# First attention of a vision tower: relu(q-k) by one add-and-clamp per four images, and matmuls in 32-column strips

## The chip, the cores and the metric

The kernel runs on one core of one Trainium2 chip. The core has five engines with a queue each: PE (TensorE, matrix products into PSUM), DVE (VectorE), ACT (ScalarE), POOL (GpSimd) and SP, which here only issues transfers. An engine takes its instructions strictly in the order in which the program gives them, and waits on semaphores for the other engines. The metric is the time of the whole program on the device in microseconds (us); the median of three runs counts.

## What is computed

The program is a small vision transformer: a tokenizer of two convolutions, a first layer (an attention and a feed-forward part that is itself an attention of experts), and a second layer (a linear attention and a mixture of experts). The change touches the first attention alone. For each of 128 images with 64 tokens of 256 features:

```python
Q = x @ Wq.T; K = x @ Wk.T; V = x @ Wv.T          # x: the layer norm of h
Qg = Q.reshape(B, L, 1, 8, 32)
Kg = K.reshape(B, 1, L, 8, 32)
diff = Qg - Kg                                     # every query against every key
attn = einsum('bqkgd,d->bqkg', relu(diff), w_mlp) + b_mlp[0]
attn = softmax(relu(attn), axis=2)                 # over the keys
out = einsum('bqkg,bkdg->bqdg', attn, Vg)
h = h + out
```

So for each image, query, key and group, 32 values relu(q - k) are weighted by `w_mlp` and summed. All is float32.

## The kernel before

`relu_attention` (L309) works on eight blocks of 16 images. In a block the features lie on the 128 partitions, in two halves (`hf`), and each image has its 64 tokens in the free dimension. A block is worked off in eight chunks of eight queries, which makes 64 chunks. For each chunk, half and image there is one part of 8 queries x 64 keys, 32 parts in all, and each must become relu(q - k) before PE sums it over features with the weights `wide` into the scores `sc` (`summed`, L340: a matmul of 32 columns, so that four images fill the four 32-row strips of `sc`).

The 32 parts are shared out by hand:

- VectorE makes 18 by `larger` (L529, the instruction is L532): max(q, k), for four images at once (2048 elements a partition, four times a chunk; the tile comes from the pool `amv` with three buffers) and once for two images (12 and 13 of half 1, 1024 elements, from `amg` with five buffers). q is read from PSUM (`pc`), broadcast over the keys; k from SBUF, broadcast over the queries.
- POOL and ACT make 12 by `difference` (L536): POOL subtracts (L540, 1024 elements, six times a chunk, `m` from `amg`), ACT clamps (L541). POOL reads a copy of q in SBUF (`queried`, L469).
- ACT makes two alone by `by_query` (L545, L550), relu(q - k) with q as the bias of one query at a time.

Since relu(q - k) = max(q, k) - k, the parts of VectorE lack a term in k. `key_sums` (L439) sums w times k over these parts once a block into `pkb`, `correction` (L449, L452) makes `kb` = b_mlp minus that sum, and `begin` (L521, L525) starts each chunk's `sc` with `kb`, by four matmuls of 32 columns with the identity as the stationary operand.

`less_max` (L562: a reduction at L566 and two more instructions, L567 and L568), `exponents`, `sums`, `weights` and `transpose` (L582, L589: 16 matmuls that turn `e` round, 64 columns each) finish the softmax of the chunk before, and lie among the steps of the present chunk. Keys (`keys`, L407), values (`values`, L426), queries (`queries`, L461) of a block are full 128-column matmuls; keys and values of the next block are made beside the chunks of the present one, each in four of eight chunks; queries are made for each next chunk.

The order of all of it is written out by hand at L696 to L757 under `manual_schedule`; `at(n, place, ...)` puts the side work (statistics and layer norm of the next block, its keys and values, the outcome of the last block with `outcome`, `back`, `added`, and in the last chunks the start of the next stage) into named places of chunk n. In one chunk VectorE has, in this order: max of images 0-3 and 4-7 of half 0, `less_max` of the chunk before, max of 0-3 of half 1, `sums`, max of 4-7 of half 1, max of 12 and 13 of half 1, and statistics. PE's sums stand behind the maxima and differences that feed them. `added` (L510) puts the result back into `h`.

Of the kernel before, what the change touches and what calls it, by code (L numbers as in the profile page):

```python
# [20 lines left out]
P = 128  # L21
B = 128
T = 64
D = 256
LN_EPS = 1e-5
BN_EPS = 1e-3
# [282 lines left out]
def relu_attention(c, sh, wqkv, wmlp, bmlp, beside):  # L309
# [10 lines left out]
    with (  # L320
# [24 lines left out]

        def direct(i, hf):

            return i // 4 == 2 or (i // 4 == 3 and (hf == 0 or i % 4 == 2))

        class Block:  # L350
# [52 lines left out]
            def keys(self, s, fo):  # L403

                self.ps["k", s, fo] = pk = sh.ps([P, 8, T], "pk")
                for fi in range(2):
                    nc.tensor.matmul(  # L407
                        pk.rearrange("p i t -> p (i t)"),
                        w[:, fi, D + fo * P : D + (fo + 1) * P],
                        self.xT[:, fi, 4 * s : 4 * s + 4, :].rearrange("p n t -> p (n t)"),  # L410
                        start=(fi == 0),
                        stop=(fi == 1),
                    )

            def keyed(self, s, fo, vector=False):
                if s == 0 and fo == 0:
                    self.k = bp.tile([P, 2, NB, T], F32, tag="k", name="k")
                copy = nc.vector.tensor_copy if vector else nc.scalar.copy
                copy(self.k[:, fo, 8 * s : 8 * s + 8], self.ps.pop(("k", s, fo)))  # L419

            def values(self, i):

                self.ps["v", i] = pv = sh.ps([P, 2, D], "pv")
                for j in range(2):
                    for fi in range(2):
                        nc.tensor.matmul(  # L426
                            pv[:, j],
                            self.xT[:, fi, 2 * i + j],
                            w[:, fi, 2 * D : 3 * D],
                            start=(fi == 0),  # L430
                            stop=(fi == 1),
                        )
# [5 lines left out]

            def key_sums(self):  # L439
                self.ps["b"] = pk = sh.ps([P, T], "pkb")  # L440
                for i0 in range(0, NB, 4):
                    for hf in range(2):
                        for i in range(i0, i0 + 4):
                            js = [(n, f) for n in range(i % 4, NB, 4) for f in range(2)]
                            js = [(n, f) for n, f in js if not direct(n // 2 * 2, f)]
                            if (i, hf) in js:
                                summed(pk, i, hf, self.k[:, hf, i], (i, hf) == js[0], (i, hf) == js[-1])

            def correction(self):  # L449

                self.kb = bp.tile([P, T], F32, tag="kb", name="kb")
                nc.vector.tensor_scalar(self.kb, self.ps.pop("b"), -1.0, bm, ALU.mult, ALU.add)  # L452

            def queries(self, q0):

                self.pc[q0] = pc = psc.tile([P, 2 * NB * 8 + 8], F32, tag="pc", name="pc")
                pq = pc[:, : 2 * NB * 8].rearrange("p (c i t) -> p c i t", c=2, i=NB)
                xi = self.xT.rearrange("p c n (b t) -> p c (n b) t", b=2)
                for fo in range(2):
                    for fi in range(2):  # L460
                        nc.tensor.matmul(  # L461
                            pq[:, fo],
                            w[:, fi, fo * P : (fo + 1) * P],
                            xi[:, fi, :, q0 : q0 + 8],
                            start=(fi == 0),
                            stop=(fi == 1),
                        )

            def queried(self, q0):  # L469
                self.q[q0] = q = ep.tile([P, 2, NB // 2, 8], F32, tag="q", name="q")  # L470
                pq = self.pc[q0][:, : 2 * NB * 8].rearrange("p (c i t) -> p c i t", c=2, i=NB)
                nc.scalar.copy(q, pq[:, :, NB // 2 :])  # L472

# [38 lines left out]
        class Chunk:  # L512


            def __init__(self, blk, q0):
                self.blk, self.q0, self.parts, self.m = blk, q0, {}, {}
                self.pc = blk.pc.pop(q0)
                self.pq = self.pc[:, : 2 * NB * 8].rearrange("p (c i t) -> p c i t", c=2, i=NB)
                self.q = blk.q.pop(q0)

            def begin(self):  # L521
                self.sc = pss.tile([P, 8, T], F32, tag="sc", name="sc")
                for j in range(0, P, 32):
                    j = slice(j, j + 32)
                    nc.tensor.matmul(  # L525
                        self.sc[j], c.ident[:, j], bcast(self.blk.kb, 1, 8), start=True, stop=False
                    )

            def larger(self, pool, i, n, hf):  # L529
                m = pool.tile([P, n, 8, T], F32, tag="m", name="m")  # L530
                k = bcast(self.blk.k[:, hf, i : i + n], 2, 8)
                nc.vector.tensor_tensor(m, bcast(self.pq[:, hf, i : i + n], 3, T), k, ALU.max)  # L532
                for j in range(n):
                    self.parts[i + j, hf] = m[:, j]

            def difference(self, i, hf):  # L536
                m = mgp.tile([P, 2, 8, T], F32, tag="m", name="m")
                s = i - NB // 2
# [22 lines left out]

            def less_max(self):  # L562
# [3 lines left out]
                nc.vector.tensor_reduce(pm, self.sc, AX.X, ALU.max)  # L566
                nc.vector.tensor_scalar_max(mx, pm, 0.0)  # L567
                nc.vector.scalar_tensor_tensor(  # L568
                    e, self.sc, 0.0, bcast(mx, 2, T), ALU.max, ALU.subtract
                )  # L570
# [11 lines left out]
            def transpose(self):  # L582
# [4 lines left out]
                for j in range(8):  # L587
                    for par in range(2):
                        nc.tensor.matmul(  # L589
                            pt[par * 64 : par * 64 + 64, j], self.e[:, j], rows[:, par], start=True, stop=True  # L590
                        )

# [34 lines left out]
        def first_rest(x):  # L627
            for s in range(2):
                x.keys(s, 1)
                x.keyed(s, 1, True)  # L630
            x.key_sums()
            x.correction()

        for b, x in enumerate(blocks):
# [43 lines left out]
            for fo in range(2):  # L678
# [3 lines left out]
                at(n - 3 + fo, "O", of(x.keyed, 1, fo))  # L682
            at(n - 2, "Y", x.key_sums)
            at(n - 1, "V1", x.correction)
            for i, (k, place) in enumerate(((6 - (b == 1), "Y"), (4, "Y"), (2, "X"), (1, "X"))):
# [10 lines left out]
        with tc.manual_schedule():  # L696
# [3 lines left out]
            for n in range(len(seq)):  # L700
                new = None
                ch.difference(8, 0)
                ch.larger(mvp, 0, 4, 0)
                do(n, "O")
                if n == 0:
                    first_rest(blocks[0])
                    ch.begin()
                ch.by_query(14, 1, 0)
                ch.add(0, 0)
                do(n, "X")  # L710
                ch.difference(10, 0)
                ch.add(8, 0)
                ch.larger(mvp, 4, 4, 0)
                ch.add(4, 0)
# [16 lines left out]
                ch.add(8, 1)  # L731
                ch.larger(mvp, 0, 4, 1)
                ch.add(0, 1)
# [6 lines left out]
                ch.by_query(15, 1, 1)  # L740
                ch.larger(mvp, 4, 4, 1)
# [12 lines left out]
                ch.add(12, 0)  # L754
                ch.add(12, 1, True)
                old, ch = ch, new
# [1655 lines left out]
```

## Time and profile before

| what | us |
|---|---|
| median of three runs (2573.55 to 2582.93) | 2578.53 |
| the profiled execution | 2578.67 |
| its span, first to last instruction | 2577.0 |
| busy in the span: PE / VectorE / ACT / POOL | 2463.2 / 2011.8 / 1631.8 / 1701.0 |
| L540, POOL, 384 differences | 719.6 |
| L532, VectorE, 320 maxima | 646.5 |
| L342, PE, 4096 records of score matmuls | 520.1 |
| L541, ACT, 384 clamps | 402.4 |
| L550, ACT, 1024 clamps by query | 270.7 |

The profile is a recording of one execution. A line of its groups gives the kernel's line, engine, operation, output and inputs, the shape, the count, then the busy time in us and the mean duration in ns, and then the idle time of the engine just before these instructions with what ended it. PE leaves two records for each float32 matmul; the ends of its records are modelled, so its busy time can hide waits, which only the starts show. PEld is the loading of the stationary operand. The stage that the change touches fills the time from about 180 to 1080 us; the rest of the span is the tokenizer before it and the other three stages behind it.

### The profile page before, as it was taken

The numbers are of one execution on the slowest core, as the hardware profiler recorded it, in microseconds if no ns is written. First come the engines' busy times: TensorE is split into PE (matmuls) and PEld (weight loads), VectorE is DVE, ScalarE is ACT, GpSimd is POOL, SyncE is SP. The second block draws the span as 40 slices with busy tenths as digits, with TensorE's granted clock in tenths as the row PEclk, the third lists the DMA queues.
The fourth block names the chain that finished last, engine by engine and source line by source line (L and its number), as shares of the span: only waits on it lengthen the run. The fifth ranks groups of instructions, "written<-read, shape, count | busy, mean of one in ns | idle before, by whom it ended". The sixth has DMA issues, their size and how long they took to land. (4 is left out here: it accounts for less than half of the span.)

```text
span 2577.0 us, 78108 instructions
## 1 busy us (share of the span) xinstructions
PE 2463.2 (96%) x33713; PEld 1623.6 (63%) x33713; DVE 2011.8 (78%) x3000; ACT 1631.8 (63%) x3421; POOL 1701.0 (66%) x1491
## 2 busy tenths in 40 slices
PE   7989999999999999899999999999999968999997
PEld 4554444444444444477777777776566547888886
DVE  5759999999999989898898889887667794444443
ACT  2228889898988888776777777775544433323332
POOL 3418989898998999787878787864232404445453
PEclk9999999999999999999999999999999989999998
DMA  3100000000000000000000000001354335555554
GB/s 113 36 13 1 2 2 2 1 2 2 2 2 2 2 2 13 2 28 14 24 14 24 14 24 14 24 14 34 84 121 110 83 89 195 181 192 191 198 190 129
DMA packets 138033, 140.97 MB, mean 55 GB/s; under 512 B 108001, under 2 KB 121859, under 8 KB 129870
## 3 DMA queue, kind: packets, MB, share of 16 engines
q1 hardware_dynamic: 128684, 119.48, 15.5%
q0 software_dynamic: 7648, 14.77, 1.8%
q8 instruction: 267, 4.37, 0.7%
q10 hardware_dynamic: 1344, 1.61, 0.2%
q14 instruction: 90, 0.74, 0.1%
HBM read 104.00 MB, written 32.54 MB: 53 GB/s over the span
## 5 line engine op out<-in xcount | busy, mean ns | idle before, releaser
L540 POOL TENSOR_TENSOR m<-q,k 128x1024 f32<-128x1024 f32 x384 | 719.6, 1908 | 55.8 <-PE sc L342 46.8
L532 DVE TENSOR_TENSOR m<-pc,k 128x2048 f32<-128x2048 f32 (+1 forms) x320 | 646.5, 2056 | 0.5 <-ACT q L472 0.5
L342 PE MATMUL sc<-m,wide 128*32 128x512 f32 x4096 | 520.1, 597 | 8.9 <-ACT m L541 6.6
L541 ACT ACTIVATE m<-m 128x1024 f32<-128x1024 f32 x384 | 402.4, 1049 | 20.5 <-POOL m L540 20.5
L342 PEld LDWEIGHTS sc<-m,wide 128*32 128x32 f32 x4096 | 134.7, 109 | 269.4 <-issue 157.7
L550 ACT ACTIVATE m<-k,q 128x64 f32<-128x64 f32 x1024 | 270.7, 338 | 0.9 <-DVE k L419 0.9
L1144 POOL TENSOR_TENSOR e<-e,mx 128x1024 f32<-128x1024 f32 x127 | 241.6, 1902 | 9.9
L2238 PE MATMUL ph<-xt,w1s 128*128 128x256 f32 x896 | 199.0, 380 | 4.4 <-ACT hT L2242 2.2
L1157 ACT COPY pT<-pt 128x512 f32<-128x512 f32 x256 | 133.4, 597 | 109.5 <-PE pt L1152 109.5
L2254 PE MATMUL po<-w2s,hT 128*128 128x256 f32 x896 | 198.0, 379 | 0.0
L2238 PEld LDWEIGHTS ph<-xt,w1s 128*128 128x128 f32 x896 | 169.8, 190 | 29.2 <-ACT hT L2242 3.4
L2254 PEld LDWEIGHTS po<-w2s,hT 128*128 128x128 f32 x896 | 168.1, 190 | 21.7
L2272 POOL DMA_INDIRECT out<-y,rout x56 | 56.6, 1010 | 168.2 <-ACT hT L2242 129.2
L1126 DVE TENSOR_REDUCE mx<-sc 128x16 f32<-128x1024 f32 x128 | 150.3, 1215 | 21.2 <-PE sc L1116 21.2
L1136 DVE TENSOR_REDUCE mx<-e 128x16 f32<-128x1024 f32 x128 | 154.7, 1209 | 6.6 <-ACT e L1133 4.9
L1133 ACT ACTIVATE e<-e 128x1024 f32<-128x1024 f32 x128 | 133.9, 1060 | 34.3 <-DVE e L1130 30.0
L2242 ACT ACTIVATE hT<-ph,w1s 128x256 f32<-128x256 f32 x224 | 93.0, 470 | 96.9 <-PE ph L2238 82.5
L2259 ACT ACTIVATE y<-y,gf 128x256 f32<-128x256 f32 x56 | 28.0, 507 | 197.3 <-issue 112.3
L1130 DVE TENSOR_TENSOR e<-sc,mx 128x1024 f32<-128x1024 f32 x128 | 150.2, 1214 | 0.1
L1041 ACT COPY kr<-pqk 128x512 f32<-128x512 f32 x248 | 127.3, 601 | 24.2 <-PE pqk L1034 24.2
L1152 PE MATMUL pt<-ident,e 128*128 128x128 f32 x1024 | 130.5, 277 | 11.0 <-POOL e L1144 9.7
L1167 PEld LDWEIGHTS pz<-pT,vr 128*64 128x64 f32 x4096 | 124.7, 138 | 21.1 <-issue 10.6
(346 smaller groups left out, 4856.5 us busy)
## 6 DMA issues: line engine op xcount, KB each, us to landing
w1s<-in_we SPq DMA_DIRECT2D x30, 1028.0 KB
w2s<-in_we SPq DMA_DIRECT2D x30, 1024.0 KB
h<-hd SPq DMA_DIRECT2D x4, 2048.0 KB
hx<-h SPq DMA_DIRECT2D x4, 2048.0 KB
out<-h SPq DMA_DIRECT2D x4, 2048.0 KB
xt<-in_x SPq DMA_DIRECT2D x15, 512.0 KB
hd<-h SPq DMA_DIRECT2D x15, 512.0 KB
x<-hd SPq DMA_DIRECT2D x12, 512.0 KB
```

What stands on the lines that cost most here:

```text
L342: nc.tensor.matmul(dst[j : j + 32], wide[:, hf, s : s + 32], part, start=start, stop=stop)
L532: nc.vector.tensor_tensor(m, bcast(self.pq[:, hf, i : i + n], 3, T), k, ALU.max)
L540: nc.gpsimd.tensor_tensor(m, bcast(self.q[:, hf, s : s + 2], 3, T), k, ALU.subtract)
L541: nc.scalar.activation(m, m, AF.Relu)
L550: nc.scalar.activation(self.parts[i, hf][:, q], self.blk.k[:, hf, i], AF.Relu, bias=self.q[:, hf, i - NB // 2, q : q + 1], scale=-1.0,)
L1126: nc.vector.tensor_reduce(mx, self.sc[x].rearrange("p h c s -> p (h c) s"), AX.X, ALU.max)
L1130: nc.vector.tensor_sub(e, self.sc[x].rearrange("p h c s -> p (h c) s"), bcast(self.sm[x], 2, T))
L1133: nc.scalar.activation(self.e[x], self.e[x], AF.Exp, scale=SCALE)
L1136: nc.vector.tensor_reduce(self.sm[x], self.e[x], AX.X, ALU.add)
L1144: eng.tensor_mul(e, e, bcast(sm, 2, T))
L2238: nc.tensor.matmul(ph[:, j], self.w1[:, w0 : w0 + P], self.xt[:, fc], start=(fc == 0), stop=(fc == 1))
L2254: nc.tensor.matmul(po, self.hT[:, f, r * P : r * P + P], self.w2[:, f, :], start=(f == 0), stop=(f == 7))
```

## The change

VectorE's maxima become an add-and-clamp, a custom instruction `TENSOR_ADD_SAT`: out = max(min(in0 + in1, s0), s1), here with s0 the largest float and s1 = 0. For that, k is kept negated (`keyed` scales by -1, POOL adds in place of subtracting, ACT's scale of -1 goes). The parts are then relu(q - k) themselves, so `key_sums`, `correction`, `kb` and `begin` go; the first score matmul of each strip starts `sc`. `relu` still takes four images, but with the images inside the queries (8 x 4 x 64), for which the queries in PSUM are laid out anew (four groups of 8 queries x 4 images). The two images that VectorE took from `amg` become two instructions of 512 elements (`relu_alone`).

The bias b_mlp, which was in `kb`, moves into the softmax: with `least` = -b_mlp, max(s, -b) less its maximum is the same as max(s + b, 0) less its maximum.

Keys, values and queries are made by `in_strips`, four matmuls of 32 columns in place of one of 128, and the transposes of `e` by 32 matmuls of 32 columns in place of 16 of 64.

```diff
+from concourse.dve_ops import TENSOR_ADD_SAT
+MOST = float(np.finfo(np.float32).max)
...
-        bm = wp.tile([P, 1], F32, name="bm")
-        nc.sync.dma_start(bm, bmlp.partition_broadcast(P))
+        least = wp.tile([P, 1], F32, name="least")
+        nc.sync.dma_start(least, bmlp.partition_broadcast(P))
+        nc.vector.tensor_scalar(least, least, -1.0, None, ALU.mult)
...
+        def in_strips(out, stationary, moving, start, stop):
+
+            for j in range(0, P, 32):
+                nc.tensor.matmul(out[j : j + 32], stationary[:, j : j + 32], moving, start=start, stop=stop)
...
             def keys(self, s, fo):
...
-                    nc.tensor.matmul(
+                    in_strips(
                         pk.rearrange("p i t -> p (i t)"),
...
             def keyed(self, s, fo, vector=False):
...
-                copy = nc.vector.tensor_copy if vector else nc.scalar.copy
-                copy(self.k[:, fo, 8 * s : 8 * s + 8], self.ps.pop(("k", s, fo)))
+                k, pk = self.k[:, fo, 8 * s : 8 * s + 8], self.ps.pop(("k", s, fo))
+                if vector:
+                    nc.vector.tensor_scalar(k, pk, -1.0, None, ALU.mult)
+                else:
+                    nc.scalar.activation(k, pk, AF.Copy, scale=-1.0)
...
             def values(self, i):
...
-                        nc.tensor.matmul(
+                        in_strips(
                             pv[:, j],
...
-            def key_sums(self):
...
-            def correction(self):
...
             def queries(self, q0):
...
-                pq = pc[:, : 2 * NB * 8].rearrange("p (c i t) -> p c i t", c=2, i=NB)
+                pq = pc[:, : 2 * NB * 8].rearrange("p (c g t i) -> p c g i t", c=2, g=4, i=4)
...
-                        nc.tensor.matmul(
+                        in_strips(
                             pq[:, fo],
...
-            def begin(self):
-                self.sc = pss.tile([P, 8, T], F32, tag="sc", name="sc")
-                for j in range(0, P, 32):
-                    j = slice(j, j + 32)
-                    nc.tensor.matmul(
-                        self.sc[j], c.ident[:, j], bcast(self.blk.kb, 1, 8), start=True, stop=False
+            def relu(self, i, hf):
+
+                m = mvp.tile([P, 8, 4, T], F32, tag="m", name="m")
+                nc.vector._custom_dve(
+                    TENSOR_ADD_SAT,
+                    out=m,
+                    in0=bcast(self.pq[:, hf, i // 4], 3, T),
+                    in1=bcast(self.blk.k[:, hf, i : i + 4], 1, 8),
+                    s0=MOST,
+                    s1=0.0,
+                )
+                for j in range(4):
+                    self.parts[i + j, hf] = m[:, :, j]
+
+            def relu_alone(self, i, n, hf):
+                m = mgp.tile([P, n, 8, T], F32, tag="m", name="m")
+                for j in range(n):
+                    nc.vector._custom_dve(
+                        TENSOR_ADD_SAT,
+                        out=m[:, j],
+                        in0=bcast(self.pq[:, hf, i // 4, :, i % 4 + j], 2, T),
+                        in1=bcast(self.blk.k[:, hf, i + j], 1, 8),
+                        s0=MOST,
+                        s1=0.0,
                     )
-
-            def larger(self, pool, i, n, hf):
-                m = pool.tile([P, n, 8, T], F32, tag="m", name="m")
-                k = bcast(self.blk.k[:, hf, i : i + n], 2, 8)
-                nc.vector.tensor_tensor(m, bcast(self.pq[:, hf, i : i + n], 3, T), k, ALU.max)
-                for j in range(n):
                     self.parts[i + j, hf] = m[:, j]
...
             def difference(self, i, hf):
...
-                nc.gpsimd.tensor_tensor(m, bcast(self.q[:, hf, s : s + 2], 3, T), k, ALU.subtract)
+                nc.gpsimd.tensor_tensor(m, bcast(self.q[:, hf, i // 4 - 2, s : s + 2], 3, T), k, ALU.add)
...
-                        bias=self.q[:, hf, i - NB // 2, q : q + 1],
-                        scale=-1.0,
+                        bias=self.q[:, hf, i // 4 - 2, i % 4, q : q + 1],
...
-            def add(self, i0, hf, last=False):
+            def add(self, i0, hf, first=False, last=False):
+                if first:
+                    self.sc = pss.tile([P, 8, T], F32, tag="sc", name="sc")
                 for i in range(i0, i0 + 4):
-                    summed(self.sc, i, hf, self.parts[i, hf], False, last)
+                    summed(self.sc, i, hf, self.parts[i, hf], first, last)
...
-                nc.vector.tensor_scalar_max(mx, pm, 0.0)
+                nc.vector.tensor_scalar_max(mx, pm, least)
                 nc.vector.scalar_tensor_tensor(
-                    e, self.sc, 0.0, bcast(mx, 2, T), ALU.max, ALU.subtract
+                    e, self.sc, least, bcast(mx, 2, T), ALU.max, ALU.subtract
                 )
...
                     for par in range(2):
-                        nc.tensor.matmul(
-                            pt[par * 64 : par * 64 + 64, j], self.e[:, j], rows[:, par], start=True, stop=True
-                        )
+                        for h in range(0, 64, 32):
+                            o = par * 64 + h
+                            nc.tensor.matmul(
+                                pt[o : o + 32, j], self.e[:, j, h : h + 32], rows[:, par], start=True, stop=True
+                            )
...
-                ch.larger(mvp, 0, 4, 0)
+                ch.relu(0, 0)
...
-                    ch.begin()
...
-                ch.add(0, 0)
+                ch.add(0, 0, first=True)
...
-                if new:
-                    new.begin()
...
-                ch.larger(mgp, 12, 2, 1)
+                ch.relu_alone(12, 2, 1)
...
```

More of the change, by code (lines that the diff above doesn't have):

```diff
@@ L344, in summed @@
             )
-        def direct(i, hf):
-            return i // 4 == 2 or (i // 4 == 3 and (hf == 0 or i % 4 == 2))
+        def in_strips(out, stationary, moving, start, stop):
+            for j in range(0, P, 32):
+                nc.tensor.matmul(out[j : j + 32], stationary[:, j : j + 32], moving, start=start, stop=stop)
         class Block:
@@ L437, in valued @@
                 nc.scalar.copy(self.v[:, 2 * i : 2 * i + 2], self.ps.pop(("v", i)))
-            def key_sums(self):
[L440 to L447, printed above, removed]
-            def correction(self):
-                self.kb = bp.tile([P, T], F32, tag="kb", name="kb")
-                nc.vector.tensor_scalar(self.kb, self.ps.pop("b"), -1.0, bm, ALU.mult, ALU.add)
             def queries(self, q0):
                 self.pc[q0] = pc = psc.tile([P, 2 * NB * 8 + 8], F32, tag="pc", name="pc")
-                pq = pc[:, : 2 * NB * 8].rearrange("p (c i t) -> p c i t", c=2, i=NB)
+                pq = pc[:, : 2 * NB * 8].rearrange("p (c g t i) -> p c g i t", c=2, g=4, i=4)
                 xi = self.xT.rearrange("p c n (b t) -> p c (n b) t", b=2)
@@ L469, in queried @@
             def queried(self, q0):
-                self.q[q0] = q = ep.tile([P, 2, NB // 2, 8], F32, tag="q", name="q")
-                pq = self.pc[q0][:, : 2 * NB * 8].rearrange("p (c i t) -> p c i t", c=2, i=NB)
-                nc.scalar.copy(q, pq[:, :, NB // 2 :])
+                self.q[q0] = q = ep.tile([P, 2, 2, 32], F32, tag="q", name="q")
+                nc.scalar.copy(q, self.pc[q0][:, : 2 * NB * 8].rearrange("p (c g u) -> p c g u", c=2, g=4)[:, :, 2:])
             def outcome(self, hf):
@@ L517, in __init__ @@
                 self.pc = blk.pc.pop(q0)
[L518 to L533 removed]
+                self.pq = self.pc[:, : 2 * NB * 8].rearrange("p (c g t i) -> p c g t i", c=2, g=4, t=8)
+                self.q = blk.q.pop(q0).rearrange("p c g (t i) -> p c g i t", i=4)
+            def relu(self, i, hf):
[20 more added lines that the diff above has]
+                        s1=0.0,
+                    )
                     self.parts[i + j, hf] = m[:, j]
@@ L537, in difference @@
                 m = mgp.tile([P, 2, 8, T], F32, tag="m", name="m")
-                s = i - NB // 2
+                s = i % 4
                 k = bcast(self.blk.k[:, hf, i : i + 2], 2, 8)
-                nc.gpsimd.tensor_tensor(m, bcast(self.q[:, hf, s : s + 2], 3, T), k, ALU.subtract)
+                nc.gpsimd.tensor_tensor(m, bcast(self.q[:, hf, i // 4 - 2, s : s + 2], 3, T), k, ALU.add)
                 nc.scalar.activation(m, m, AF.Relu)
@@ L630, in first_rest @@
                 x.keyed(s, 1, True)
-            x.key_sums()
-            x.correction()
         for b, x in enumerate(blocks):
@@ L682, in relu_attention @@
                 at(n - 3 + fo, "O", of(x.keyed, 1, fo))
-            at(n - 2, "Y", x.key_sums)
-            at(n - 1, "V1", x.correction)
             for i, (k, place) in enumerate(((6 - (b == 1), "Y"), (4, "Y"), (2, "X"), (1, "X"))):
@@ L712, in relu_attention @@
                 ch.add(8, 0)
-                ch.larger(mvp, 4, 4, 0)
+                ch.relu(4, 0)
                 ch.add(4, 0)
@@ L731, in relu_attention @@
                 ch.add(8, 1)
-                ch.larger(mvp, 0, 4, 1)
+                ch.relu(0, 1)
                 ch.add(0, 1)
@@ L740, in relu_attention @@
                 ch.by_query(15, 1, 1)
-                ch.larger(mvp, 4, 4, 1)
+                ch.relu(4, 1)
                 ch.add(4, 1)
-                if new:
-                    new.begin()
                 if old:
@@ L754, in relu_attention @@
                 ch.add(12, 0)
-                ch.add(12, 1, True)
+                ch.add(12, 1, last=True)
                 old, ch = ch, new
```

## The prediction

> **What bounds the kernel now.** I read the busy time by window first, for the stage that the diff touches: 64 chunks, from the first max of L532 at 194.6 us to the end of the last at 1078.9 us, or 13.8 us a chunk. One block of eight chunks:
>
> ```profile
> core 0: us, PE busy (x) PEld busy (x) DVE busy (x) ACT busy (x) POOL busy (x), PEclk, DMA share, GB/s
> 526.00:636.00 110.00, 109.49 (x1268) 49.98 (x1267) 103.93 (x101) 98.96 (x225) 100.94 (x65) 1.00 0.01 2
> ```
>
> PE is busy for 13.69 us of a chunk's 13.75, VectorE for 12.99, POOL 12.62, ACT 12.37. A busy PE need not be a working one, so next comes the timeline of PE over one chunk.
>
> ```profile
> 501.82 1.22 PE L525 MATMUL sc<-kb,ident 128*32 128x512 f32 x8
> 502.97 1.15 PE L589 MATMUL pt<-ident,e 128*64 128x64 f32 x32
> 504.06 1.98 PE L407 MATMUL pk<-xT,w 128*128 128x512 f32 x4
> 505.97 2.78 PE L342 MATMUL sc<-m,wide 128*32 128x512 f32 x24
> 508.68 1.99 PE L426 MATMUL pv<-w,xT 128*128 128x256 f32 x8
> 510.61 1.92 PE L342 MATMUL sc<-m,wide 128*32 128x512 f32 x16
> 512.46 1.16 PE L461 MATMUL pc<-xT,w 128*128 128x128 f32 x8
> 513.55 0.70 PE L342 MATMUL pkb<-k,wide 128*32 128x64 f32 x34
> ```
>
> Each matmul of the program leaves two records. No step waits for data: the 24 records of L342 are six groups of four 32-column strips running at once, and 6 x 0.43 us = 2.58 fills the 2.71 us until the next step. PE really is full. What remains are 0.13 to 0.29 us at each change of matmul width. Now VectorE: its groups by form, and a piece of its timeline.
>
> ```profile
> L532 DVE TENSOR_TENSOR m<-pc,k 128x2048 f32<-128x2048 f32 x256 | 574.8, 2266 | 0.5 <-ACT q L472 0.5
> L532 DVE TENSOR_TENSOR m<-pc,k 128x1024 f32<-128x1024 f32 x64 | 77.7, 1214 | 0.0
> L566 DVE TENSOR_REDUCE pc<-sc 128x8 f32<-128x512 f32 x64 | 44.5, 696 | 37.5 <-PE sc L342 37.1
> L568 DVE SCALAR_TENSOR_TENSOR e<-sc,mx 128x512 f32<-128x512 f32 x64 | 44.3, 692 | 2.4 <-DVE mx L567 0.2
> L147 DVE SCALAR_TENSOR_TENSOR h<-pa,s,ev 128x512 f32<-128x512 f32 x32 | 22.4, 742 | 0.7 <-POOL ev L230 0.7
> L510 DVE TENSOR_TENSOR h<-h,pto 128x512 f32<-128x512 f32 x32 | 21.5, 677 | 0.2 <-PE pto L500 0.2
> L452 DVE TENSOR_SCALAR kb<-pkb,bm 128x64 f32<-128x64 f32 x8 | 2.2, 276 | 0.4 <-PE pkb L342 0.4
> ```
>
> ```profile
> 502.15 4.46 DVE L532 TENSOR_TENSOR m<-pc,k 128x2048 f32<-128x2048 f32 x2
> 507.99 0.70 DVE L566 TENSOR_REDUCE pc<-sc 128x8 f32<-128x512 f32 x1 [1.38 <-PE sc L342]
> 508.79 0.17 DVE L567 TENSOR_SCALAR mx<-pc 128x8 f32<-128x8 f32 x1
> 508.99 0.69 DVE L568 SCALAR_TENSOR_TENSOR e<-sc,mx 128x512 f32<-128x512 f32 x1
> 509.60 2.28 DVE L532 TENSOR_TENSOR m<-pc,k 128x2048 f32<-128x2048 f32 x1
> 511.80 0.68 DVE L576 TENSOR_REDUCE mx<-e 128x8 f32<-128x512 f32 x1
> ```
>
> VectorE loses 37.1 us to PE over the run, nearly all at L566, which needs the old chunk's last score matmuls. Everything else it does back to back, and more than that: L532 at 509.60 ends at 511.88, yet L576 starts at 511.80. A long instruction's successor starts about 0.08 us before the record of the first ends; one that needs its predecessor's result (L568 after L567) starts 0.03 us after it. Without its waits a VectorE chunk takes 12.84 us between starts (525.77 to 538.61 in the trace), plus extras in some chunks.
>
> **The change on PE.** Removed: L525, eight records in two groups of four, 2 x 0.43 = 0.86 us a chunk, and the pkb sums, about 0.6 us a block, 0.07 a chunk. Width changes go where the groups become strips: 0.13 before and 0.20 after the queries (513.55 - 512.46 = 1.09 against 8 x 0.11 of streaming), the same around values and keys, which each come in half of the chunks, and 0.29 before the transposes of e. So 0.33 + 0.33 + 0.29. The strips cost no streaming: L525 is itself four strips with one moving operand, and ran four at once. Weight loads and starts quadruple, but the pkb records, 64 columns long, follow each other at 56 ns per group of four. At that pace the e transposes' 64 records take 16 x 0.056 = 0.90 us against 1.09 now: 0.19 less. In sum 0.86 + 0.07 + 0.95 + 0.19 = 2.07, and PE falls from 13.69 to 11.6 us a chunk. It stops being the bound. The transposes of xn and oT and the 64-row outcome matmuls stay as they are. `m` is now read in runs of 64 with a stride; the queries read runs of eight and lose 0.005 of 0.11 us, so I count nothing.
>
> **The change on VectorE,** the next in line. Its total work becomes the bound, so its waits are the most that can be won.
> - The wait at L566 goes with PE's load: -37.1 us. Where a little stays (chunks with outcome or back-transposes load PE more, and POOL and ACT feed it late) I put +4 back.
> - L452 goes: 8 x 0.276 = -2.2. The one sign flip of `least` waits for the DMA that fed `bm`, and stands behind the xT copies, ahead of the first k copy: VectorE idled 3.44 us there for PE. The load is issued at 185.2 us and VectorE's k copy starts at 193.4, so it has 8 us of cover: nothing; each us that it lands later would cost one.
> - The add-and-clamp does not occur in the trace. It streams as many elements, so 2.05 of the 2.27 us (twice the 1.05 us between the 1024 and 2048 rows) should stay; what is open is its fixed part. Bounds at 512 elements with a PSUM input: 677 ns for the plain L510, 742 for L147. In between L568, 692 ns, two operations in one pass from PSUM: I take that, 15 ns over plain. On 256 large ones: +3.8 us.
> - The 1024-element max becomes two of 512: 2 x (692 - 83) = 1218 against 1214 - 83 = 1131 ns, 64 times: +5.6.
> - keyed with a sign flip: same size and engine; nothing. Pointer `least` in place of 0.0 in two small instructions: nothing, the row L147 has one too (it is inside its 742).
>
> Sum: -37.1 + 4 - 2.2 + 3.8 + 5.6 = -25.9 us on a span of 2577.0; with 1.7 us outside it, 2552.8 for that execution. It took 2578.67, 0.14 over the median, so I say 2552.5. Per chunk VectorE then has 13.4 us against 12.6 of POOL and 12.4 of ACT, whose own work does not change.
> Ends: with the plain 677 and no wait left, 2 x 594 - 1131 = 57 ns x 64 = 3.7, so -35.6: 2543. With L147's price, +65 ns on 256 and 2 x 659 - 1131 = 187 ns on 64: +16.6 + 12 - 35.3 = -6.7: 2572. Below nothing: were the fixed part of the large ones (2266 - 2 x 1052 = 162 ns, 83 of it overlapped) gone, 20 us more, but POOL's 12.6 with its gaps then binds near 13: about 2530.
>
> **The rivals.**
> 1. *The new instruction does not overlap its neighbour (slower).* If each add-and-clamp starts 34 ns after its predecessor instead of 83 before, that is 117 ns x 6 x 64 = 45 us on VectorE: -25.9 + 44.9 = +19, 2597. It decides from 25.9 / 384 = 67 ns of extra fixed cost. For it: no such instruction is in the trace. Against it: L568, a different kind with two operations, overlaps too (508.99 + 0.69 = 509.68, and its successor starts at 509.60). The Trainium skill (VectorE: DVE Perf Modes, "Two Vector instructions with no wait between them") has an instruction held back only when an operand starts in another group of 32 partitions than before; by that rule this one, starting at partition 0 like its neighbours, keeps its overlap, and the rows above agree.
> 2. *POOL and ACT take over.* Both stay above 12.3 us, in order, and POOL's L540 waits 46.8 us in all for `m` buffers that PE gives back. If the three engines still trade waits, half of VectorE's 37 stays: -25.9 + 14.5 = -11, 2567.
> 3. *No gain:* the fixed cost meets those 67 ns: 2572 to 2586.
> 4. *The strips do not run side by side.* With two of four at once, queries, the e transposes and the halved keys and values cost about 0.9 us more each: 11.6 + 3.5 = 15.1 us on PE, 1.35 more than now, times 64: 2665. L525 speaks against it.
> 5. *VectorE and POOL block each other.* It happens here:
>
> ```profile
> 64.25 6.87 POOL L161 TENSOR_TENSOR v<-h 128x1536 f32<-128x1536 f32 x2 [9.51 <-PE pc L184]
> 68.69 2.98 DVE L217 SCALAR_TENSOR_TENSOR h<-z,n 128x512 f32<-128x512 f32 x1
> ```
>
> L217 takes 0.75 us otherwise; it ends when POOL does. Its two tensors are both in SBUF. If the add-and-clamp were caught like that, 2.2 us x 384 = 850 us: about 3400. L532 reads PSUM and SBUF, as the new one does, and ran beside POOL undisturbed. The Trainium skill (GPSIMD Engine Reference, "Specifications") says that POOL shares its SBUF interfaces with VectorE and contends with instructions that have two SBUF inputs or a two-port mode; by that rule the new one is free, and the trace agrees for L217 and L532.
>
> **Chances.** Forecast 0.66; POOL and ACT 0.10; no gain 0.07; overlap lost 0.12; strips 0.03; ports 0.02. The measurement tells 0.3% (7.7 us) from no change: below 2570.8 is faster. Forecast and rival 2 give faster 0.76, rival 3 the 0.07, the rest slower 0.17. The likeliest case has 2543 to 2572; the range runs from 2535, where the fixed part shrinks, to 2590, half way into rival 1.
>
> **What would show it.** Right: in a block's window PE near 85 to 90% and VectorE at 98% or more; L566 with under 5 us of waiting; the relu at 2.25 to 2.33 us per 2048 and 0.68 to 0.75 per 512, starts overlapping; strips in groups of four, 0.43 us apart; chunks of 13.3 to 13.5 us. Wrong: a relu over 2.35 us or starts after the predecessor's end (rival 1), a new wait of VectorE or PE on ACT or POOL above 10 us (2), PE still without idle time (4), a relu that ends with a POOL instruction (5).

## The result and the profile after

The changed kernel takes 2558.46 us (median of four runs, 2556.08 to 2559.22); the kernel before, run in turn with it, 2576.59 (four runs, 2573.55 to 2582.93). The ratio is 0.9921, with a 95% interval from 0.9902 to 0.9940: faster by 0.8%. The profiled execution took 2559.22 us with a span of 2557.5, 19.5 less than the span before. Cut at the first and the last max (now add-and-clamp) of VectorE, the two profiled spans come apart like this:

| stretch of the span, us | before | after | difference |
|---|---|---|---|
| ahead of the stage | 194.6 | 195.6 | +1.0 |
| the stage: 64 chunks | 884.3 | 859.9 | -24.4 |
| behind it | 1498.1 | 1502.0 | +3.9 |

The first view is the busy time by window over the whole stage, before and then after. The columns are the window, its length, and the busy time of each engine with its count of instructions.

```profile
core 0: us, PE busy (x) PEld busy (x) DVE busy (x) ACT busy (x) POOL busy (x), PEclk, DMA share, GB/s
194.60:1078.85 884.25, 874.76 (x9946) 398.52 (x9946) 835.70 (x819) 786.49 (x1779) 812.52 (x526) 1.00 0.01 3
```

```profile
core 0: us, PE busy (x) PEld busy (x) DVE busy (x) ACT busy (x) POOL busy (x), PEclk, DMA share, GB/s
195.58:1055.50 859.92, 821.96 (x13772) 404.61 (x13764) 843.13 (x875) 781.06 (x1779) 824.73 (x526) 1.00 0.01 3
526.00:636.00 110.00, 106.50 (x1806) 52.74 (x1798) 108.26 (x112) 101.54 (x232) 105.97 (x67) 1.00 0.01 2
```

Read VectorE: it idled 884.25 - 835.70 = 48.6 us and now idles 16.8, which is 31.8 less, while its work grew by 7.4. The difference of the two is the 24.4 us of the stage. In the block's window VectorE is busy for 98.4% of the time. PE still looks 97% busy although it now waits (30.9 us for ACT, in the last line of the next view); its real load shows in the starts, further down.

Next the groups by form in the changed kernel: five of VectorE, then one each of POOL and PE.

```profile
L515 DVE CUSTOM_DVE_ANT_1 m<-pc,k 128x2048 f32<-128x2048 f32 x256 | 574.7, 2266 | 0.5 <-ACT q L463 0.5
L529 DVE CUSTOM_DVE_ANT_1 m<-pc,k 128x512 f32<-128x512 f32 x128 | 81.7, 680 | 0.0
L572 DVE SCALAR_TENSOR_TENSOR e<-sc,least,mx 128x512 f32<-128x512 f32 x64 | 48.1, 751 | 2.4 <-DVE mx L571 0.2
L570 DVE TENSOR_REDUCE pc<-sc 128x8 f32<-128x512 f32 x64 | 44.2, 691 | 6.0 <-PE sc L345 5.8
L571 DVE TENSOR_SCALAR mx<-pc,least 128x8 f32<-128x8 f32 x64 | 14.5, 226 | 6.7
...
L543 POOL TENSOR_TENSOR m<-q,k 128x1024 f32<-128x1024 f32 x384 | 732.1, 1946 | 15.0 <-ACT q L463 8.9 <-PE sc L345 6.1
...
L345 PE MATMUL sc<-m,wide 128*32 128x512 f32 x4096 | 589.6, 600 | 36.3 <-ACT m L544 30.9 <-DVE m L515 3.5 <-issue 0.4
```

The wait of the reduction for PE fell from 37.1 us to 5.8 (L566 before, L570 now). The large add-and-clamp costs 2266 ns, to the nanosecond what the max cost. Two prices rose that nobody touched on purpose: L572 from 692 to 751 ns and L571 from 167 to 226, 59 ns each, the two instructions that now take `least` where 0.0 stood. POOL's difference rose from 1908 to 1946. PE has turned from the engine that others wait for into one that waits, for ACT's part of the differences.

One chunk on PE and on VectorE in the timeline of the changed kernel (start, length, engine, line):

```profile
482.82 2.93 PE L345 MATMUL sc<-m,wide 128*32 128x512 f32 x24
485.40 2.07 PE L352 MATMUL pk<-xT,w 128*32 128x512 f32 x16
487.11 2.07 PE L345 MATMUL sc<-m,wide 128*32 128x512 f32 x16
488.83 1.12 PE L352 MATMUL pc<-xT,w 128*32 128x128 f32 x30
489.71 0.60 PE L345 MATMUL sc<-m,wide 128*32 128x512 f32 x2
```

```profile
480.59 4.45 DVE L515 CUSTOM_DVE_ANT_1 m<-pc,k 128x2048 f32<-128x2048 f32 x2
484.96 0.69 DVE L570 TENSOR_REDUCE pc<-sc 128x8 f32<-128x512 f32 x1
485.76 0.23 DVE L571 TENSOR_SCALAR mx<-pc,least 128x8 f32<-128x8 f32 x1
486.02 0.75 DVE L572 SCALAR_TENSOR_TENSOR e<-sc,least,mx 128x512 f32<-128x512 f32 x1
486.69 2.28 DVE L515 CUSTOM_DVE_ANT_1 m<-pc,k 128x2048 f32<-128x2048 f32 x1
488.89 0.68 DVE L580 TENSOR_REDUCE mx<-e 128x8 f32<-128x512 f32 x1
```

On PE the keys in strips take 487.11 - 485.40 = 1.71 us, four groups of four at 0.43, where the full-width keys took 1.91 (504.06 to 505.97 before); the queries 0.88 from start to start where it was 1.09. The strips do run four at once. On VectorE nothing waits any more: L570 starts 0.08 us before the record of its predecessor ends, and L580 stands to the add-and-clamp at 486.69 in the same way (486.69 + 2.28 = 488.97 against 488.89).

### The profile page after: what moved, and what is told of

It reads as the page before. It is cut to its first block, busy times and chain, and to the rows that moved or that the text cites. A ratio compares the mean times of both kernels' runs of the same rounds, so it can differ in the third digit from the quotient of the medians.

```text
span 2557.5 us, 86015 instructions
## 1 busy us (share of the span) xinstructions
PE 2412.5 (94%) x37649; PEld 1631.0 (64%) x37649; DVE 2020.5 (79%) x3057; ACT 1626.8 (64%) x3421; POOL 1714.5 (67%) x1491
## 5 line engine op out<-in xcount | busy, mean ns | idle before, releaser
L543 POOL TENSOR_TENSOR m<-q,k 128x1024 f32<-128x1024 f32 x384 | 732.1, 1946 | 15.0 <-ACT q L463 8.9
L345 PE MATMUL sc<-m,wide 128*32 128x512 f32 x4096 | 589.6, 600 | 36.3 <-ACT m L544 30.9
L515 DVE CUSTOM_DVE_ANT_1 m<-pc,k 128x2048 f32<-128x2048 f32 x256 | 574.7, 2266 | 0.5 <-ACT q L463 0.5
L544 ACT ACTIVATE m<-m 128x1024 f32<-128x1024 f32 x384 | 403.2, 1051 | 27.9 <-POOL m L543 27.4
L345 PEld LDWEIGHTS sc<-m,wide 128*32 128x32 f32 x4096 | 163.4, 109 | 308.9 <-issue 119.3
L2241 ACT ACTIVATE hT<-ph,w1s 128x256 f32<-128x256 f32 x224 | 93.2, 471 | 98.4 <-PE ph L2237 95.9
L2258 ACT ACTIVATE y<-y,gf 128x256 f32<-128x256 f32 x56 | 28.0, 506 | 194.8 <-issue 109.2
```

Of the source, the lines that this page charges most:

```text
L345: nc.tensor.matmul(dst[j : j + 32], wide[:, hf, s : s + 32], part, start=start, stop=stop)
L515: nc.vector._custom_dve(TENSOR_ADD_SAT, out=m, in0=bcast(self.pq[:, hf, i // 4], 3, T), in1=bcast(self.blk.k[:, hf, i : i + 4], 1, 8), s0= ...
L543: nc.gpsimd.tensor_tensor(m, bcast(self.q[:, hf, i // 4 - 2, s : s + 2], 3, T), k, ALU.add)
```

## The experiments

All are made from the changed kernel unless said otherwise; the ratio is to the kernel before, run in the same series. The series differ (the kernel before had 2576.59, then 2581.03 beside e1 to e4 and 2580.02 beside e5 to e8), so medians compare within a series. The stage alone reproduces far better than the whole time: the changed kernel in a later series (e5) had a stage of 859.9 us, 0.02 from the first. So the stage is the measure for what lies inside it.

| kernel | median us | ratio, 95% interval | stage us | behind it us |
|---|---|---|---|---|
| before | 2576.59 | | 884.3 | 1498.1 |
| changed | 2558.46 | 0.9921, 0.9902 to 0.9940 | 859.9 | 1502.0 |
| e1 strips alone | 2568.92 | 0.9953, 0.9937 to 0.9969 | 874.3 | 1499.4 |
| e2 relu alone | 2567.97 | 0.9950, 0.9937 to 0.9963 | 869.8 | 1504.2 |
| e3 no pointer | 2555.58 | 0.9902, 0.9887 to 0.9917 | 855.1 | 1505.0 |
| e4 q from SBUF, one run | 2687.64 | | 987.1 | 1503.2 |
| e5 changed, again | 2557.83 | 0.9908, 0.9891 to 0.9924 | 859.9 | 1502.9 |
| e6 PE kept busy | 2555.01 | 0.9905, 0.9888 to 0.9921 | 860.0 | 1495.7 |
| e7 q by image | 2553.97 | 0.9894, 0.9877 to 0.9910 | 858.6 | 1505.6 |
| e8 three edits | 2552.07 | 0.9889, 0.9873 to 0.9906 | 855.7 | 1496.7 |

### e1: the strips without the add-and-clamp

The kernel before, with keys, values and queries through `in_strips` and the transposes of `e` in 32 columns; the max, the key sums and `begin` stay.

```diff
-                    nc.tensor.matmul(
+                    in_strips(
...
-                        nc.tensor.matmul(
-                            pt[par * 64 : par * 64 + 64, j], self.e[:, j], rows[:, par], start=True, stop=True
-                        )
+                        for h in range(0, 64, 32):
+                            o = par * 64 + h
+                            nc.tensor.matmul(
+                                pt[o : o + 32, j], self.e[:, j, h : h + 32], rows[:, par], start=True, stop=True
+                            )
```

> The kernel before, with the 32-column strips for keys, values, queries and the transposes of e, but with max(q,k), begin and the corrections kept. Theory (before, PE was the bound by a little; after, VectorE is, and the add-and-clamp adds to VectorE): PE falls from 13.7 to about 12.5 us a chunk, which is already under VectorE's 13.2 (12.84 a chunk, 0.3 of added() and correction), so this is faster than the changed kernel, which carries 0.19 us a chunk more on VectorE: 2540 to 2552 us, L566's wait under 8 us. Rival (the gain needs the removal of begin): PE stays the bound in the chunks with outcome and back, and the time lies between, 2560 to 2570.

### e2: the add-and-clamp without the strips

The changed kernel with full-width matmuls and the transposes of `e` as before: the lines of e1 the other way round.

> The changed kernel, with full-width matmuls for keys, values and queries and 64-column transposes of e as before. Theory: PE has 13.7 - 0.93 = 12.8 us a chunk, VectorE 13.35; VectorE is the bound in most chunks, PE in those with outcome or back: 2560 to 2568. Rival 1 (the strips bring nothing): 2557 to 2560, as the changed kernel. Rival 2 (the strips bring nearly all): 2572 or more.

Each alone gave about half of the gain: 2568.92 and 2567.97, with 2581.03 before. For e1 the theory fell: its reduction L571 still waits 27.9 us for PE, where under 8 were expected, and the time lies in the rival's range. The time of e2 lies in the range of its theory. Both texts, though, had named the chunks with outcome and back as those in which PE stays the longest, and the table below shows it above all for the chunks with keys, 21 and 22. The stage lost 10.0 us in e1, 14.5 in e2, 24.4 with both. Chunk by chunk (lengths in us, from VectorE's first max or relu of one chunk to that of the next, one block):

| chunk, and its side work on PE | before | e1 | e2 | changed |
|---|---|---|---|---|
| 20: keys, values | 12.84 | 12.84 | 13.03 | 13.03 |
| 21: keys twice | 14.91 | 13.76 | 13.60 | 13.04 |
| 22: keys, values | 14.32 | 13.75 | 13.61 | 13.03 |
| 23: values | 13.14 | 13.15 | 13.11 | 13.11 |
| 24: none | 12.84 | 12.84 | 13.03 | 13.03 |
| 25: outcome | 12.99 | 12.84 | 13.03 | 13.03 |
| 26: values, back, `added` | 14.33 | 15.81 | 14.32 | 14.33 |
| 27: back, `added` | 14.91 | 14.81 | 14.23 | 14.22 |

Chunk 21 in windows, e1 first, then e2:

```profile
485.80:499.50 13.70, 13.70 (x208) 7.64 (x202) 12.67 (x13) 12.78 (x31) 12.21 (x8) 1.00 0.01 2
```

```profile
484.20:497.90 13.70, 13.70 (x118) 5.66 (x118) 13.00 (x15) 12.81 (x31) 12.54 (x8) 1.00 0.01 2
```

PE has no idle time in either, and VectorE has. So the kernel before was bound by PE in some chunks and by VectorE (12.84 us) in others (in 23, 24 and 26 POOL had no idle time either, before and after), and each half of the change still leaves PE the longest in chunks 21 and 22. The theory for e1 had set the mean load of PE against the mean of VectorE; but the engines work in order with few buffers, and a chunk's slack does not pay for its neighbour. The halves shorten chunk 21 by 1.15 and 1.31 us, which together would put PE at 14.91 - 2.46 = 12.45 us, an estimate, below VectorE's 13.03; there VectorE takes over.

Chunk 26 of e1 is 1.5 us longer than before. Just ahead of it, from 549.88 to 551.67 us, PE stops in the 64 small matmuls of `outcome`, waiting for nothing that the profile shows; this happens in every second block, and in the blocks on either side, without such a stop, the same chunk takes 14.16 us (groups by form on PE, 200 to 1050 us, before and e1):

```profile
L482 PE MATMUL po<-at,v 64*32 64x64 f32 x1792 | 20.8, 225 | 0.0
```

```profile
L487 PE MATMUL po<-at,v 64*32 64x64 f32 x1792 | 21.5, 225 | 5.0 <-issue 5.0
```

Here the changed kernel has 1.6 us of it and e2 none. Yet it does not need the strips: the kernel before stops in the same way in its last `outcome`, just behind the stage:

```profile
1090.92 1.52 PE L482 MATMUL po<-at,v 64*32 64x64 f32 x128 [0.76 <-issue]
1094.66 0.38 PE L482 MATMUL po<-at,v 64*32 64x64 f32 x17 [2.22 <-issue]
```

No experiment was made on its cause; the traces show this much. Queue q8, which the pages call "instruction", moves packets of 16,384 bytes, one for every 126 matmul records of PE (267 packets and 33713 records before, 298 and 37649 after). Between 200 and 2000 us the ten traces hold 62 stops of PE of over 0.6 us that the profile puts down to issue, and every one of them ends 1.2 to 1.7 us after such a packet has landed; by chance 7 to 8% would. That fits PE waiting for the next piece of its program. It is a coincidence in time, not a test.

### e3: 0.0 in place of `least`

This leaves out the bias b_mlp.

```diff
-                nc.vector.tensor_scalar_max(mx, pm, least)
+                nc.vector.tensor_scalar_max(mx, pm, 0.0)
...
-                    e, self.sc, least, bcast(mx, 2, T), ALU.max, ALU.subtract
+                    e, self.sc, 0.0, bcast(mx, 2, T), ALU.max, ALU.subtract
```

> The changed kernel, with the constant 0.0 in place of the pointer scalar least in the two instructions of less_max; the bias b_mlp is left out of the scores. Theory (VectorE without gaps is the bound): the two instructions fall back from 226 to 167 and from 751 to 692 ns, 0.12 us a chunk, 7.6 us over 64: 2549 to 2552. Rival (another engine is as close, and takes the place): less than 3 us, 2555 to 2559.

Both instructions went back to their old prices (groups by form of VectorE in e3, 190 to 1060 us):

```profile
L572 DVE SCALAR_TENSOR_TENSOR e<-sc,mx 128x512 f32<-128x512 f32 x64 | 44.3, 692 | 2.4 <-DVE mx L571 0.2
...
L571 DVE TENSOR_SCALAR mx<-pc 128x8 f32<-128x8 f32 x64 | 10.7, 167 | 6.7
```

A chunk bound by VectorE shrank from 13.03 to 12.91 us, by the whole 2 x 59 ns. The stage lost 4.8 us, between the 7.6 (64 x 0.118) of the theory and the 3 of its rival, because in some chunks something else is the longest by then. Chunk 26, first in the changed kernel, then in e3:

```profile
545.80:560.10 14.30, 13.91 (x204) 6.02 (x200) 14.07 (x16) 12.71 (x29) 14.30 (x9) 1.00 0.01 2
```

```profile
542.70:557.30 14.60, 13.54 (x204) 5.93 (x200) 14.03 (x17) 12.65 (x29) 14.60 (x9) 1.00 0.01 2
```

POOL is busy without a gap in both, and the chunk grew by 0.2 us while VectorE's work shrank.

### e7: POOL's copy of q laid out by image again

The changed kernel's copy keeps the new order, in which the eight queries of an image lie four elements apart. Here ACT's copy turns it round, so that POOL reads them in a row.

```diff
-                nc.scalar.copy(q, self.pc[q0][:, : 2 * NB * 8].rearrange("p (c g u) -> p c g u", c=2, g=4)[:, :, 2:])
+                pq = self.pc[q0][:, : 2 * NB * 8].rearrange("p (c g t i) -> p c g i t", c=2, g=4, i=4)
+                nc.scalar.copy(q, pq[:, :, 2:])
...
-                self.q = blk.q.pop(q0).rearrange("p c g (t i) -> p c g i t", i=4)
+                self.q = blk.q.pop(q0)
```

> The changed kernel, with ACT's copy of q laid out by image again (queries next to each other), PSUM as changed. Theory (POOL's subtraction went from 1908 to 1946 ns because its q is now read with a stride of four elements): 1908 ns again, ACT's copy within 50 ns of 253; as VectorE is the bound, at most 2 us faster. Rival (POOL is slower because VectorE now leaves it less of SBUF): 1946 ns stays.

```profile
L544 POOL TENSOR_TENSOR m<-q,k 128x1024 f32<-128x1024 f32 x384 | 718.7, 1909 | 16.4 <-ACT q L464 8.8 <-PE sc L345 7.5
```

That is POOL's group in e7: 1909 ns against 1946, and 1908 before the change. So the stride is the cause of those 38 ns, 14.6 us of POOL's time over the run. The stage gained only 1.3 us, within the 2 us expected: of the eight chunks of a block POOL is without idle time in 23, 24 and 26; 24 is no longer than VectorE's own 13.03 us, and the other two shrank by 0.04 and 0.06 us. The whole times can't tell it from e5 (0.9894 and 0.9908, intervals overlapping).

### e6: PE kept busy where the stage ends

Behind the stage the changed kernel lost 3.9 us although nothing there was edited. The windows of 20 us around the end of the stage, changed and then before (the third column from the right is the granted clock):

```profile
1040.00:1060.00 20.00, 17.15 (x308) 7.46 (x300) 16.61 (x21) 13.85 (x31) 12.61 (x9) 0.91 0.01 2
1060.00:1080.00 20.00, 14.78 (x563) 12.62 (x564) 12.50 (x17) 9.29 (x16) 7.10 (x9) 0.74 0.02 3
```

```profile
1063.30:1083.30 20.00, 17.21 (x256) 7.59 (x248) 16.59 (x20) 14.18 (x32) 12.74 (x9) 1.00 0.01 2
1083.30:1103.30 20.00, 15.48 (x667) 13.60 (x668) 14.53 (x20) 9.99 (x18) 7.43 (x9) 0.91 0.02 4
```

Narrower windows read 0.50, so PE ran at half clock for about 2 x 20 x (0.09 + 0.26) = 14 us here, from 1051.5 to 1054.9 and from 1068.5 to 1078.7 us (the expectation below has these stretches about 10 us too late), against some 4 before. e6 adds matmuls without use around the end of the 64th chunk, into PSUM tiles that are written over or not read.

```diff
+                for x in po:
+                    c.busy(x.rearrange("p a b -> p (a b)")[:, 0:P], c.ident, idle)
...
+                c.busy(pt.rearrange("p a b -> p (a b)")[:, 0:P], c.ident, idle)
...
+                if n == len(seq) - 1:
+                    c.busy(psc.tile([P, 2 * NB * 8 + 8], F32, tag="pc", name="idle")[:, 0:P], c.ident, 10)
...
-        chunk.transpose()
+        chunk.transpose(6)
...
-        last.outcome(0)
-        last.outcome(1)
+        last.outcome(0, 4)
+        last.outcome(1, 6)
```

> The changed kernel, with small idle matmuls at four places where PE waits around the end of the 64th chunk (10 in the last chunk, 6 before the last transposes of e, 4 and 6 per tile before the last outcome matmuls; their results are overwritten). Theory (4 us of the stage's gain are lost behind it because PE, now idle more, runs at half clock from 1062 to 1065 and from 1079 to 1089 us): no half clock between 1040 and 1100, the next stage starts some 23 us earlier than before as the 64th chunk does, and the time falls by 3 to 4 us. Rival (the half clock is a mark of the waits and costs nothing, or the idle matmuls delay the real ones by as much): within 1 us of the changed kernel.

> The changed kernel once more, as the mark for the others of this call. Theory and rivals alike: 0.99 to 0.994 of the kernel before.

```profile
1040.00:1060.00 20.00, 18.68 (x332) 9.64 (x324) 16.65 (x21) 14.21 (x33) 13.08 (x9) 1.00 0.01 2
1060.00:1080.00 20.00, 18.90 (x686) 16.68 (x687) 13.72 (x20) 9.93 (x17) 6.13 (x7) 1.00 0.02 4
```

In e6 the clock stays full, as the theory said. Its time, 2555.01, is 2.8 us under the 2557.83 of e5 (0.9908 of the kernel before, as expected), with overlapping runs. Whether the clock is what was won shows farther back. ACT runs the same 3421 instructions in every kernel, so its work can be matched instruction by instruction, each counted from its own kernel's end of the stage. The work 206 us behind it stands, against before, 4.5 us later in the changed kernel and 1.6 in e5, the same program; 0.6 to 3.0 later in the other kernels without idle matmuls (e4 0.6, e1 1.9, e2 2.3, e7 2.7, e3 3.0); and 0.3 earlier in e6 and 0.6 in e8, the two with them.

But the two do not win it where the idle matmuls stand. Up to 78 us behind the stage e6 is 1.2 us late and e8 0.9, no better than e5 (1.2) or e7 (0.8): here the rival holds. At 80 us they are 2.1 us ahead of that, because of a stop. First the changed kernel, then e5, then e6:

```profile
1139.52 0.27 PE L957 MATMUL pl<-oTr,xTr 128*32 128x128 f32 x1 [1.81 <-issue]
1139.72 1.63 PE L1182 MATMUL po<-xTr,z 128*128 128x256 f32 x4
1141.28 3.13 PE L1166 MATMUL pz<-pT,vr 128*64 128x64 f32 x64
```

```profile
1137.34 0.27 PE L957 MATMUL pl<-oTr,xTr 128*32 128x128 f32 x1 [1.82 <-issue]
1137.54 1.13 PE L1182 MATMUL po<-xTr,z 128*128 128x256 f32 x4
1138.60 2.09 PE L1166 MATMUL pz<-pT,vr 128*64 128x64 f32 x64
```

```profile
1136.05 0.64 PE L962 MATMUL pl<-oTr,xTr 128*32 128x128 f32 x16
1136.62 1.13 PE L1187 MATMUL po<-xTr,z 128*128 128x256 f32 x4
```

All eight kernels without idle matmuls, the one before too, stop here for 1.5 to 2.1 us in the matmuls into `pl`, in the way of the stops of e1; e6 and e8 do not stop. Behind the stop, the changed kernel, e2, e3 and e7 run 3.4 us at half clock, as `pz` with 3.13 us in place of 2.09 shows, and fall back by another 1.6 us; before, e1, e4 and e5 keep the full clock. So half clock does cost time there, but the theory of e6, that the full clock at the end of the stage wins 3 to 4 us, is not shown; that the idle matmuls move the places at which PE stops would fit, and was not tested. Farther back the profiles drift apart by several us in parts that no kernel changes.

### e4: q from SBUF in the small add-and-clamps

```diff
-                        in0=bcast(self.pq[:, hf, i // 4, :, i % 4 + j], 2, T),
+                        in0=bcast(self.q[:, hf, i // 4 - 2, i % 4 + j], 2, T),
```

> The changed kernel, with the two 512-element add-and-clamps reading q from ACT's copy in SBUF in place of PSUM, so that both tensors are in SBUF. Theory (VectorE with two SBUF tensors waits for POOL's running instruction, as L217 did in the tokenizer): they take 1 to 2.7 us each in place of 0.68, VectorE's chunk grows by 1 to 4 us, 2620 to 2800 us. Rival (the long L217 had another cause): 0.70 to 0.75 us, the time within 5 us of the changed kernel.

The same two groups in e4:

```profile
L529 DVE CUSTOM_DVE_ANT_1 m<-q,k 128x512 f32<-128x512 f32 x128 | 201.5, 1614 | 0.0
```

```profile
L543 POOL TENSOR_TENSOR m<-q,k 128x1024 f32<-128x1024 f32 x384 | 771.6, 2044 | 12.6 <-ACT q L463 9.0 <-PE sc L345 3.5
```

With both inputs in SBUF the instruction of 680 ns takes 1614 in the mean, and POOL's 2044 in place of 1946. The mean hides two kinds: 36 of the 128 take 0.68 us as before, and the other 92 take 0.89 to 2.43 us, and every one of these ends 0.55 us after an instruction of POOL has ended. 128 x 0.934 = 120 us, and the stage grew by 127: the theory held. The Trainium skill (GPSIMD Engine Reference, "Specifications") has VectorE and POOL contend when a VectorE instruction has two inputs in SBUF; the trace agrees for this instruction too.

### e8: the three edits together

e6 and e7 together, and the max against `least` as an instruction with two tensors:

```diff
-                nc.vector.tensor_scalar_max(mx, pm, least)
+                nc.vector.tensor_tensor(mx, pm, least.to_broadcast([P, 8]), ALU.max)
```

> The changed kernel with the idle matmuls, q by image, and the maximum against least as a two-tensor instruction with a broadcast in place of a pointer scalar (226 to about 173 ns). Theory: 3.5 us from the clock, 3.4 us from 64 x 53 ns, about 1 us from POOL, so 7 to 9 us under the changed kernel, near 0.989 of the kernel before. Rival (each of them is hidden): less than 2 us.

```profile
L575 DVE SCALAR_TENSOR_TENSOR e<-sc,least,mx 128x512 f32<-128x512 f32 x64 | 48.1, 751 | 2.4 <-DVE mx L574 0.2
...
L574 DVE TENSOR_TENSOR mx<-pc,least 128x8 f32<-128x8 f32 x64 | 10.7, 167 | 6.5
```

The max is back at 167 ns with the bias kept (the other pointer, in L575, stays at 751). The stage is 855.7 us, 4.2 less than e5's. The median is 5.8 us under e5's, less than the 7 to 9 of the theory and more than the 2 of its rival. With 2552.07 (2548.66 to 2552.70) every run of e8 lies below every run of the changed kernel, here and in e5; the interval of its ratio, 0.9873 to 0.9906, still overlaps that of e5.

## Why the prediction held, and where it did not

Time: 2552.5 was said and 2558.46 came, on a before that measured 1.9 us lower in this series. The fall of the profiled span was forecast as 25.9 and was 19.5. By the steps:

- *PE bounds the kernel, and falls below VectorE.* Right in mechanism. The forecast's PE terms give a chunk with two key steps 1.47 (3 x 0.33 + 0.29 + 0.19, strips and transposes) and 0.86 (`begin`); e1 and e2 measured 1.15 and 1.31 of relief there: each term is off, and the sum of 2.46 is near 2.33. What the text did not see is that VectorE waits for PE in three of eight chunks only (21, 22 and 27), and that the mean of 13.75 us is made of chunks of 12.84 to 14.9. The sum did not suffer, because it was made with VectorE's waits, which already count chunk by chunk.
- *The wait at L566, -37.1 + 4.* It left 5.8, a little more than the 4 and than the 5 of the sign: -31.3.
- *L452, -2.2.* Gone, as said.
- *The large add-and-clamp, +3.8.* Nothing: 2266 ns, like the max. The row taken for it, L568 at 692 ns, was too dear; the plain L510 (677) was near, as the 680 of the small one shows too.
- *Two of 512 for one of 1024, +5.6.* The pair takes 1195 ns from start to start against 1131: 64 ns x 64 = +4.1.
- *Pointer `least`, nothing.* This step failed, and is the largest error within the stage: 59 ns in each of two instructions, +7.6 us over 64 chunks. The row L147 with its 742 ns, a like operation with a pointer against 692 for L568, had shown most of it; the text named the pointer in it and still wrote nothing. e3 shows that 4.8 us of it lie on the path.
- *The strided queries, nothing.* True for PE, but the same layout cost POOL 38 ns x 384, which the text did not look for; 1.3 us of it reach the stage (e7).
- *Outside the stage, nothing.* +1.0 ahead and +3.9 behind. The first is scatter: in e5, the same program, the stage begins at 194.8. The second is a loss whose size the traces do not settle: the seven traces of kernels with an edit and without idle matmuls have 1499.4 to 1505.6 us behind the stage, against 1498.1 in the only one of the kernel before. By ACT's work 206 us on, the changed kernel had lost 4.5 us and e5 1.6; up to 78 us they had lost 2.7 and 1.2, with 13.6 and 6.8 us at half clock against 3.4 before, and another 1.6 us of the difference is the half clock behind the stop at `pl`. No run shows how to win this back with certainty.

In the stage these terms give -31.3 - 2.2 + 4.1 + 7.6 = -21.8 against the measured -24.4; 0.5 of the rest is idle time at other lines; the other 2.1 would fit the overlap of instructions that no longer wait and so start 0.08 us inside their predecessor's record. The forecast of -25.9 for the stage was thus near by luck: it put the two kinds of add-and-clamp 5.3 us too high, the pointer 7.6 and the wait 1.8 too low, and 2.6 us of the gain belong to no term of it. Of the 6.4 us between the forecast and the span, 4.9 were lost outside the stage.

The rivals: *overlap lost* is out (486.69 + 2.28 against 488.89), *no gain* too. *Strips not side by side* is out by 1.71 us for the keys. *Ports* is out for the change as made, and e4 shows that the price was real; its sign, a relu that ends with a POOL instruction, was read a little wrong, since L217 too ended 0.55 us after POOL (71.67 against 71.12). *POOL and ACT take over* came in part: PE now waits 30.9 us for ACT, the sign named for this rival, yet harmlessly in the block shown, where VectorE idles only 0.2 us in each of the eight chunks; and POOL is full in chunk 26; the forecast's 12.6 us for POOL was a mean, too. Chunks of 13.3 to 13.5 us came only as a mean (six of 13.0 to 13.1, two of 14.2 to 14.3). The sign "PE at 85 to 90%" failed, since the records cover its waits; the starts would have been the sign to name.

## What to carry to other kernels

Where engines work in order with few buffers, compare their loads chunk by chunk and not by the mean: each of two edits to the bound engine brought 0.5%, and only both together brought it below the next engine in the heavy chunks. Cost every operand that changes from a constant to a pointer, and every layout that another engine also reads, from a row that has it, however small the instruction. When an engine stops being the bound, look at what it does at the edges of the stage: the changed kernel's PE had 13.6 us at half clock there against 3.4 before. And where a kernel gets faster or slower in a part that nobody touched, match its instructions one by one until the step is found: what looked like the clock in e6 was for 2.1 us a stop of PE that was missing.

## What the runs showed of the hardware

- A pointer scalar costs VectorE 59 ns in an instruction of 8 elements and in one of 512 alike (167 to 226, 692 to 751); as a broadcast second tensor it costs nothing (167).
- The custom add-and-clamp runs at the pace of a plain two-tensor instruction (2266 ns like the max at 2048 elements, 680 against 677 for L510 at 512), and overlaps its successor by the same 0.08 us.
- A VectorE instruction with both tensors in SBUF can wait for the POOL instruction that runs: in e4, 92 of 128 ended 0.55 us after one, with up to 2.43 us in place of 0.68.
- POOL's time depends on the stride of a broadcast operand: 1946 ns with four elements between queries, 1908 with one.
- PE fell to half clock at about 1051.5 us in the changed kernel, after a gap of 2.34 us, the longest in its stage, as its timeline has it (24 records, usually 2.8 us, took 5.44):

```profile
1045.94 1.92 PE L345 MATMUL sc<-m,wide 128*32 128x512 f32 x16
1050.20 5.44 PE L345 MATMUL sc<-m,wide 128*32 128x512 f32 x24 [2.34 <-ACT m L544]
```

  The gap alone does not decide: e5, the same program, had the same gap of 2.34 us there and a granted clock of 1.00. The Trainium skill (TensorE: Matmul & The Clock Gate, "What's actually happening") asks for an idle window of some 3.4 us; the records show no gap that long here, though their modelled ends may hide part of one.
- PE can stop for 0.6 to 3.2 us with no wait in the profile, in runs of small matmuls above all, before the change as after; each of the 62 stops counted under e1 ends 1.2 to 1.7 us after a packet of 16,384 bytes on the instruction queue has landed. The cause is not tested.
